# A four-layer graph network: the diagonal out of layer 1's gather lists, and layer 2 written between layer 1's blocks

## The chip, the cores and the metric

The kernel runs on one core of a Trainium2 chip. Times are device microseconds of one execution. Beside the timed runs there is one execution that the hardware profiler took; all durations of single instructions come from it.

## What is computed

Four residual layers over a graph of 2708 nodes with 128 features each, every one closed by a layer norm. `adj` is a 2708 x 2708 matrix of which some 0.6% of the entries are non-zero (16 per row on average); its diagonal is always filled.

```python
# layer 0: neighbours' mean, weighted
x = ln(x + (adj.T @ x) / adj.sum(axis=0)[:, None])
# layer 1: one message per pair (i, j), weighted by adj, then an update
s, d = x @ msg_w[:, :D].T, x @ msg_w[:, D:].T
agg = einsum('ijd,ij->id', gelu(s[:, None] + d[None] + msg_b), adj)
h = gelu(concat([x, agg], -1) @ upd_w.T + upd_b) + x
x = ln(x + ln(h))
# layer 2: a product with adj, batch statistics over the nodes, leaky relu
h = adj @ (x @ W) + b
x = ln(x + leaky(gamma * (h - h.mean(0)) * rsqrt(h.var(0) + eps) + beta))
# layer 3: four attention heads, scores masked and weighted by adj, row sums to one
x = ln(x + concat(heads(x, adj)) @ w)
```

The messages of layer 1 and the scores of layer 3 are needed only where `adj` is not zero.

## The kernel before

The nodes stand in 22 blocks of rows: 21 of 128 and one of 20.

**Layer 0 and the search.** `load` brings a block's rows (128 x 2708 numbers, 1.39 MB) through SP's queue into a ring of nine slots. `count_and_sum` counts the non-zeros of each row on ScalarE (two passes with an accumulated sum: signs, L401, and negatives, L404) and multiplies the block with x on TensorE (L411), summing over all blocks in six PSUM banks. `extract` finds the non-zero entries of the rows on VectorE: the eight largest of each of 16 segments (L435) with their places (L430), and from these 128 candidates the 32 largest, eight at a time. The first 13 blocks (`SPLIT`) are searched during layer 0, the other nine, the second group, during layer 1. The order of VectorE's instructions is written by hand up to the end of layer 0, and that of TensorE, VectorE and ScalarE in layer 3. In between, a planner of the language orders each engine's instructions: by their place in the text, and by when it expects their inputs to be ready.

**Lists.** `lists` turns the found keys into values and column numbers, `ranking` orders the nodes of a group by their number of neighbours, and `place` scatters the list of each node to its rank in an HBM table (`lists_dram`; GpSimd). `sorted_lists` reads them back, so that block b of layer 1 holds nodes of similar degree, and `CAPS[b]` bounds the length of the longest list in it. A wrong bound or an overfull list is counted in `wrong`, which chooses a dense path at the very end.

**Layer 1.** Layer 0 leaves x in `x1_dram` and d (with its bias) in `d_dram`. For each of the 22 sorted blocks `own_row` gathers the nodes' own x; `messages` gathers, for each place k of the lists, the row of d that place k names for each of the 128 nodes (one GpSimd instruction for each k, L237, into one of five buffers for up to eight of them), adds s, applies gelu and sums, weighted, on VectorE (L813, L816, L824); `update` does the rest, scatters the result to `x2_dram` and leaves x W of the block in SBUF (`xw`).

**Transposition.** Layer 2 sums over the columns of `adj`, in layer 1's order. So `transposed` turns each block of rows on TensorE (L877), evicts four 128 x 128 pieces at a time on ScalarE (L882, three buffers) and writes them to `at_dram` through SP's queue (L884): 154 writes. The second group's rows are still in the ring; the first group's are loaded again. In the text the second group is transposed after its search, one block after each block of layer 1 from block 0 on; the first group after blocks 9 to 12.

**Layer 2** stands after the loop. For each sorted block it gathers 128 rows of `at_dram` (GpSimd, into the ring) and multiplies them with `xw` on TensorE (L929), in six banks. Batch statistics, layer norm and the tables of layer 3 follow, then layer 3 over 24 blocks and 100 quads of gathers.

Of the kernel before, what the change touches and what calls it, by code (L numbers as in the profile page):

```python
# [9 lines left out]
FP = mybir.dt.float32  # L10
# [5 lines left out]
P = 128  # L16
# [18 lines left out]

SLOTS = 32
# [6 lines left out]
CAPS = [32, 24, 21, 20, 19, 18, 17, 16, 16, 15, 14, 13, 12, 31, 22, 20, 18, 17, 16, 14, 13, 10]  # L43
# [36 lines left out]
def gnn_resnorm_kernel(  # L80
# [123 lines left out]
    x1_dram = tables.tile([NBLK * P, D], FP, name="x1_dram")  # L204
    d_dram = tables.tile([NBLK * P, D], FP, name="d_dram")
# [10 lines left out]
    wrong = keep.tile([P, NBLK, 4], FP, name="wrong")  # L216
# [19 lines left out]
    def gather(dst, table, index):  # L236
        nc.gpsimd.indirect_dma_start(  # L237
            out=dst,
            out_offset=None,
            in_=table[0:N, :],  # L240
            in_offset=bass.IndirectOffsetOnAxis(ap=index, axis=0),
        )
# [85 lines left out]
    with ExitStack() as layer:  # L328
# [9 lines left out]
        nc.gpsimd.memset(cnt, 0.0)  # L338
        k1 = work.tile([P, NBLK, SLOTS], FP, name="k1")
# [58 lines left out]
        def count_and_sum(b, rows):  # L398
            r0, n = BLOCKS[b]
            junk = work.tile([P, N], I8, name="junk")  # L400
            nc.scalar.activation(  # L401
                junk[0:n, :], rows[0:n, :], AF.Sign, accum_out=cnt[0:n, b : b + 1]
            )
            nc.scalar.activation(  # L404
                junk[0:n, :], rows[0:n, :], AF.Relu, scale=-1.0,
                accum_out=wrong[0:n, b, 0:1],
            )
            for jb in ORDER:
                j0, m = BLOCKS[jb]
                for k, c0, f0, f1 in acc_parts(jb):  # L410
# [7 lines left out]
                    started.add(k)  # L418

# [94 lines left out]
        def lists(b0, b1):  # L514

            nb = b1 - b0
            shape = [P, nb, SLOTS]
# [4 lines left out]
            v1 = k1[:, b0:b1, :]  # L522
            nc.vector.tensor_copy(rows[:, :, 2 * SLOTS], cnt[:, b0:b1])
            nc.vector.tensor_copy(rows[:, :, 2 * SLOTS + 1], node[:, b0:b1])
            nc.vector.tensor_copy(code, k2[:, b0:b1, :])
# [5 lines left out]
            cols = rows[:, :, SLOTS : 2 * SLOTS]  # L531
# [7 lines left out]
            nc.vector.tensor_tensor(rows[:, :, 0:SLOTS], v1, seg.bitcast(FP), ALU.mult)  # L539
# [16 lines left out]
        def sorted_lists(g):  # L556
# [3 lines left out]
            for c0, c1, n in parts:  # L560
# [6 lines left out]
                nc.vector.tensor_copy(idx[0:n, c0:c1, :], ls[0:n, c0:c1, SLOTS : 2 * SLOTS])  # L567
# [25 lines left out]
        def spread(b, po, c0):  # L593
# [23 lines left out]
            nc.vector.tensor_scalar(bad[0:n], node3[0:n, b, 0:1], float(c), None, ALU.is_gt)  # L617
# [44 lines left out]
        for b in range(RING):  # L662
            take(b)
        for b in range(SPLIT):
# [39 lines left out]
        def layer0(b0, count, n):  # L704
# [32 lines left out]
            for j in range(count):  # L737
# [6 lines left out]
                x1_dram[b0 * P : b0 * P + w, :].rearrange("(b p) w -> p b w", p=n),  # L744
# [10 lines left out]
            for j in range(count):  # L755
# [10 lines left out]
                d_dram[b0 * P : b0 * P + w, :].rearrange("(b p) w -> p b w", p=n),  # L766
# [24 lines left out]
        def own_row(b):  # L791
            n = BLOCKS[b][1]
            x_s = mine.tile([P, D], FP, name="x_s", bufs=3)
# [1168 lines left out]
```

## Times and profile before

| | us |
|---|---|
| median of 3 runs (lowest to highest) | 1979.47 (1973.92 to 1994.36) |
| the profiled execution | 1674.75 |
| its span, first to last instruction | 1673.0 |
| layer 0: from the start to its last matmul | 190.5 |
| end of layer 0, tables of x and d | 190.5 to 224 |
| layer 1 with the transpositions and the first part of layer 2 | 224 to 831 |
| rest of layer 2's product | 831 to 882 |
| layer 2's statistics, tables of layer 3 | 882 to 951 |
| layer 3 | 951 to 1673 |

The stages overlap at their edges; the bounds are the last layer-0 matmul, the first gather of layer 1, the last gather before GpSimd falls idle, the last layer-2 matmul and the last scatter of layer 2's result. In the profile a gather or scatter is one GpSimd instruction named DMA_INDIRECT: its time is the time to issue, and the data land later. A matmul in float32 appears as two records. The granted clock is TensorE's, as a share of full speed.

### The profile page before, as it was taken

How to read it: one execution, taken by the hardware profiler on the slowest of the kernel's cores; microseconds unless marked ns; L12 is line 12 of the kernel's file. 1: busy time of each engine (PE TensorE's matmuls, PEld its weight loads, DVE VectorE, ACT ScalarE, POOL GpSimd, SP SyncE). 2: the span in 40 equal slices, each digit the busy share in tenths (PEclk: the TensorE clock that was granted, in tenths of full speed). 3: DMA queues.
4: the chain of work that ended last, by engine and by line, in shares of the span. 5: the costliest groups of instructions: out<-in, count | busy, mean ns of one | idle time of the engine just before them, and what ended most of it. 6: DMA issues, size and time to landing. Idle time of an engine off the chain costs nothing. (4 is left out here: it accounts for less than half of the span.)

```text
span 1673.0 us, 24020 instructions
## 1 busy us (share of the span) xinstructions
PE 1197.2 (72%) x5876; PEld 850.9 (51%) x5876; DVE 1215.7 (73%) x5697; ACT 695.7 (42%) x2635; POOL 916.7 (55%) x1007
## 2 busy tenths in 40 slices
PE   5996654455626544463795769988989988998994
PEld 5996543334414533463684325554555555555553
DVE  9999966777747571455444479788889888898883
ACT  4959543433314120111111534454545545554552
POOL 0000247777775677777610578665656666666530
PEclk9997555555555666686796856776677777767675
DMA  9433277798937524342531687976666766867630
GB/s 352 179 128 123 50 213 170 206 230 239 258 90 181 168 60 117 119 148 84 190 138 45 201 273 206 233 215 190 192 191 203 214 190 166 231 190 221 190 92 8
DMA packets 162245, 288.49 MB, mean 172 GB/s; under 512 B 44342, under 2 KB 115890, under 8 KB 155015
## 3 DMA queue, kind: packets, MB, share of 16 engines
q0 software_dynamic: 61120, 191.23, 40.8%
q1 hardware_dynamic: 95893, 90.69, 17.5%
q10 hardware_dynamic: 5082, 4.94, 1.0%
q8 instruction: 49, 0.80, 0.2%
q14 instruction: 101, 0.83, 0.2%
HBM read 242.74 MB, written 43.97 MB: 171 GB/s over the span
## 5 line engine op out<-in xcount | busy, mean ns | idle before, releaser
L237 POOL DMA_INDIRECT g<-t_dram,idx x400 | 402.3, 1006 | 195.1 <-issue 133.4
L237 POOL DMA_INDIRECT msg<-d_dram,idx x398 | 376.9, 947 | 124.6 <-issue 103.6
L1254 ACT ACTIVATE sum_junk<-g 126x128 bf16<-126x128 f32 (+3 forms) x800 | 235.3, 296 | 117.0 <-DVE g L1246 66.1
L929 PE MATMUL acc<-x_nat,at_rows 128*128 128x128 f32 (+2 forms) x968 | 155.5, 318 | 119.9 <-DMA at_rows<-at_dram,perm 119.9
L1223 PE MATMUL z<-x,copies 32*126 32x512 f32 (+3 forms) x800 | 212.3, 887 | 30.4 <-DVE g L1423 29.7
L877 PE MATMUL pt_a<-ident,rows 128*128 128x128 f32 (+1 forms) x484 | 115.6, 393 | 145.8 <-ACT at_sb L882 145.6
L929 PEld LDWEIGHTS acc<-x_nat,at_rows 128*128 128x128 f32 (+2 forms) x968 | 140.0, 225 | 130.7 <-DMA at_rows<-at_dram,perm 110.8
L1423 DVE TENSOR_TENSOR g<-g,z 126x1536 f32<-126x1536 f32 (+3 forms) x100 | 174.9, 1749 | 11.5 <-PE z L1223 11.3
L877 PEld LDWEIGHTS pt_a<-ident,rows 128*128 128x128 f32 (+1 forms) x484 | 82.3, 202 | 173.1 <-ACT at_sb L882 172.0
L411 PE MATMUL acc<-x_nat,rows 128*128 128x129 f32 (+5 forms) x1188 | 155.1, 290 | 18.5 <-DMA rows<-in_adj_dram 18.5
L1228 PE MATMUL z<-g,ident 126*126 126x512 f32 (+3 forms) x200 | 166.2, 926 | 0.0
L411 PEld LDWEIGHTS acc<-x_nat,rows 128*128 128x128 f32 (+2 forms) x1188 | 148.8, 207 | 24.5 <-DMA rows<-in_adj_dram 19.3
L1254 ACT ACTIVATION_READ_ACCUMULATOR sum_junk<-g 126x1 f32 (+3 forms) x800 | 149.6, 187 | 0.0
L1300 PEld LDWEIGHTS po_s<-wm,g 126*128 126x128 f32 (+3 forms) x800 | 119.4, 233 | 43.3 <-DVE wm L1287 32.1
L1300 PE MATMUL po_s<-wm,g 126*128 126x24 f32 (+6 forms) x800 | 121.3, 306 | 25.2 <-DVE wm L1287 23.4
L824 DVE SCALAR_TENSOR_TENSOR own<-msg,ls,own 128x128 f32<-128x128 f32 (+1 forms) x310 | 108.1, 349 | 37.9 <-ACT msg L816 36.5
L813 DVE TENSOR_TENSOR msg<-msg,own 128x1024 f32<-128x1024 f32 (+4 forms) x58 | 61.8, 1065 | 95.3 <-PE own L804 63.6
L245 POOL DMA_INDIRECT lists_dram<-lists,rank x22 | 21.5, 978 | 183.0 <-DVE cv L435 162.5
L1246 DVE SCALAR_TENSOR_TENSOR g<-g,a_ps 126x1024 f32<-126x1024 f32 (+3 forms) x100 | 121.2, 1212 | 0.2 <-issue 0.2
L882 ACT COPY at_sb<-pt_a 128x512 f32<-128x512 f32 (+3 forms) x154 | 69.5, 479 | 116.4 <-DMA at_dram<-at_sb 112.3
L430 DVE FIND_INDEX8 ci<-cv,rows 128x8 uint32<-128x170 f32 (+1 forms) x352 | 114.7, 326 | 0.0
L435 DVE MAX8 cv<-rows 128x8 f32<-128x170 f32 (+1 forms) x352 | 110.8, 318 | 0.0
(283 smaller groups left out, 2135.6 us busy)
## 6 DMA issues: line engine op xcount, KB each, us to landing
rows<-in_adj_dram SPq DMA_DIRECT2D x34, 1354.0 KB
at_dram<-at_sb SPq DMA_DIRECT2D x105, 256.0 KB
g<-t_dram,idx POOLq DMA_INDIRECT x400, 4.6
msg<-d_dram,idx POOLq DMA_INDIRECT x398, 3.0
t_dram<-t_row SPq DMA_DIRECT2D x21, 256.0 KB
at_dram<-at_sb SPq DMA_DIRECT2D x21, 64.0 KB
x_dram<-x_nat SPq DMA_DIRECT2D x5, 256.0 KB
d_dram<-d_sb SPq DMA_DIRECT2D x5, 256.0 KB
```

The source lines that it names most:

```text
L237: nc.gpsimd.indirect_dma_start(out=dst, out_offset=None, in_=table[0:N, :], in_offset=bass.IndirectOffsetOnAxis(ap=index, axis=0),)
L411: nc.tensor.matmul(accs0[k][0:m, c0 : c0 + f1 - f0], lhsT=rows[0:n, j0 : j0 + m], rhs=x_nat[0:n, b, f0:f1], start=k not in started, stop=( ...
L430: nc.vector.max_index(out=ci[0:n, at], in_max=cv[0:n, at], in_values=rows[0:n, c0 : c0 + cw])
L435: nc.vector.max(out=cv[0:n, 8 * s : 8 * s + 8], in_=rows[0:n, c0 : c0 + cw])
L877: nc.tensor.transpose(pt[0:m, j, 0:n], rows[0:n, c0 : c0 + m], ident[0:n, 0:n])
L929: nc.tensor.matmul(accs2[ib // 4][0:m, (ib % 4) * D : (ib % 4 + 1) * D], lhsT=at[0:n, i0 : i0 + m], rhs=xw[0:n, b, :], start=(b == 0 and i ...
L1223: nc.tensor.matmul(z3[0:e, r, :] if r < 3 else z1[0:e], lhsT=copies[g][rows, j, :], rhs=own[b][1][rows, :], start=True, stop=r < 3, skip_g ...
L1228: nc.tensor.matmul(z1[0:e], lhsT=ident[0:e, 0:e], rhs=g4[0:e, 3, 0:HD], start=False, stop=True, skip_group_check=True,)
L1246: nc.vector.scalar_tensor_tensor(z, z, 0.0, a_ps[0:e].unsqueeze(1).to_broadcast((e, 2, HD)), ALU.max, ALU.mult)
L1254: nc.scalar.activation(junk[0:e], g4[0:e, r, hd * D : (hd + 1) * D], AF.Identity, accum_out=sc[0:e, r, hd : hd + 1],)
L1300: nc.tensor.matmul(po[:, p0 * HEADS : (p0 + g) * HEADS], lhsT=g4s[i][0:e, r, HD : HD + D], rhs=wm[0:e, 4 * i + r, :, :], start=True, stop= ...
L1423: nc.vector.tensor_tensor(z, z, z3[0:e], ALU.add)
```

## The change

It has three parts.

1. The diagonal leaves the lists. `count_and_sum` first multiplies the diagonal block of the rows, then sets its diagonal to zero on GpSimd (`affine_select`) and only then counts; `extract` finds one entry less per row. The diagonal's values are read from HBM by a DMA of single elements on ScalarE's queue (`diag`), and `lists` puts them into place 0, with the node itself as the column. In layer 1 the message of place 0 needs no gather: x and d of a node now stand side by side in one table, `dx_dram`, so the gather of the own row brings d along; the other gathers read the same table as rows of half the length, with doubled numbers. `CAPS` now bounds the lists without the diagonal.
2. `transposed` comes before `extract` for the second group and puts the diagonal back: for the diagonal block two accumulated matmuls, the cleared block and a diagonal matrix made on ScalarE. The first group's blocks are reloaded and transposed one after each layer-1 block from the second on, two after blocks 9 to 11.
3. Layer 2's product moves into layer 1's loop: from block 11 on, up to two of its blocks after each `update`; only the last stands behind the loop.

Besides there is a check that no diagonal entry is negative.

```diff
-CAPS = [32, 24, 21, 20, 19, 18, 17, 16, 16, 15, 14, 13, 12, 31, 22, 20, 18, 17, 16, 14, 13, 10]
+CAPS = [30, 22, 20, 19, 18, 17, 16, 15, 15, 14, 13, 12, 10, 29, 20, 18, 17, 16, 14, 13, 12, 8]
...
-            for jb in ORDER:
+            for jb in [b, *(jb for jb in ORDER if jb != b)]:
...
+                if jb == b:
+                    nc.gpsimd.affine_select(
+                        out=rows[0:n, j0 : j0 + m], in_=rows[0:n, j0 : j0 + m],
+                        compare_op=ALU.not_equal, fill=0.0, base=0,
+                        pattern=[[-1, m]], channel_multiplier=1,
+                    )
+            junk = work.tile([P, N], I8, name="junk")
+            nc.scalar.activation(
+                junk[0:n, :], rows[0:n, :], AF.Sign, accum_out=cnt[0:n, b : b + 1]
+            )
...
             take(b)
+            if b == 3:
+                line = adj[0:1, 0:1]
+                for b0, count, n in ((0, NFULL, P), (NFULL, 1, NREM)):
+                    nc.scalar.dma_start(
+                        diag[0:n, b0 : b0 + count],
+                        bass.AP(
+                            tensor=line.tensor, offset=line.offset + b0 * P * (N + 1),
+                            ap=[[N + 1, n], [P * (N + 1), count], [1, 1]],
+                        ),
+                    )
...
-            x_s = mine.tile([P, D], FP, name="x_s", bufs=3)
-            gather(x_s[0:n, :], x1_dram, perm[0:n, b : b + 1])
+            x_s = mine.tile([P, 2, D], FP, name="x_s", bufs=3)
+            gather(
+                x_s[0:n].rearrange("p t d -> p (t d)"), dx_dram, perm[0:n, b : b + 1]
+            )
...
+            mk = x_s[0:n, 0, :]
+            nc.vector.tensor_tensor(mk, mk, s_ps[0:n], ALU.add)
+            nc.scalar.activation(mk, mk, AF.Gelu)
+            weigh(0, mk)
+            for c0, c1 in chunks_of(kk):
...
                 for k in range(kc):
-                    gather(msg[0:n, k, :], d_dram, idx[0:n, b, c0 + k : c0 + k + 1])
+                    gather(
+                        msg[0:n, k, :], dx_dram.rearrange("n (t d) -> (n t) d", t=2),
+                        idx[0:n, b, c0 + k + 1 : c0 + k + 2], rows=2 * N,
+                    )
...
+            if cleared:
+                back = small.tile([P, P], FP, name="back")
+                nc.scalar.activation(back, ident, AF.Copy, scale=diag[:, b : b + 1])
...
+                    if cleared and j0 + j == b:
+                        for i, part in enumerate((rows[0:n, c0 : c0 + m], back[0:n, 0:m])):
+                            nc.tensor.matmul(
+                                pt[0:m, j, 0:n], lhsT=part, rhs=ident[0:n, 0:n],
+                                start=(i == 0), stop=(i == 1),
+                            )
...
+        def layer2(b):
+
+            n = BLOCKS[b][1]
+            at = ring.tile([P, N], FP, name="at_rows", tag="rows")
+            gather(at[0:n, :], at_dram, perm[0:n, b : b + 1])
+            for ib in range(NBLK) if b == 0 else ORDER:
+                i0, m = BLOCKS[ib]
+                nc.tensor.matmul(
+                    accs2[ib // 4][0:m, (ib % 4) * D : (ib % 4 + 1) * D],
+                    lhsT=at[0:n, i0 : i0 + m],
+                    rhs=xw[0:n, b, :],
+                    start=(b == 0 and ib % 4 == 0),
+                    stop=(b == NBLK - 1 and ib in (3, 7, 11, 15, 19, 20)),
+                )
...
                     e = left.pop(0)
+                    transposed(e, rows_of[e], True)
                     run(extract(e, rows_of[e]))
-                    transposed(e, rows_of[e])
...
             update(b, x_s, x_st, agg)
-            if not left and b >= 9:
-                for e in range(4 * (b - 9), min(SPLIT, 4 * (b - 8))):
+
+            for _ in range(2 if b in (9, 10, 11) else 1):
+                if b and again:
+                    e = again.pop(0)
                     transposed(e, load(e))
-
-
-        accs2 = banks("acc2_")
-        for b in range(NBLK):
...
+            if b == 11:
+                accs2.extend(banks("acc2_"))
+            if b >= 11:
+                for e in range(2 * (b - 11), min(b, 2 * (b - 10))):
+                    layer2(e)
+        layer2(NBLK - 1)
```

## The prediction

> **What bounds the kernel now.** I read the windows first, by stage, then GpSimd's timeline in the stage that the change is about, then TensorE's and VectorE's at that stage's two ends. The chain of waits is of no use: it holds only the last scatter. A line of the windows gives the stretch, its length, busy time and count of TensorE, its weight loads, VectorE, ScalarE and GpSimd, then granted clock, DMA share and GB/s.
>
> ```profile
> 0.00:190.50 190.50, 155.24 (x1192) 148.85 (x1193) 185.11 (x1075) 137.63 (x121) 15.34 (x71) 0.91 0.47 175
> ...
> 224.00:515.00 291.00, 142.46 (x611) 109.78 (x610) 195.78 (x1030) 108.29 (x248) 217.85 (x229) 0.56 0.78 204
> 515.00:831.00 316.00, 164.24 (x912) 144.89 (x911) 162.17 (x745) 62.35 (x157) 224.79 (x238) 0.67 0.44 126
> 831.00:882.00 51.00, 50.65 (x378) 44.85 (x377) 23.00 (x109) 8.28 (x27) 7.31 (x11) 0.94 0.40 159
> ```
>
> Layer 0 (to 190 us) is VectorE's: 185 of 190. Layer 1 (224 to 831) seems only 71 to 75% GpSimd's, but its timeline leaves no room between gathers:
>
> ```profile
> 641.46 0.95 POOL L237 DMA_INDIRECT msg<-d_dram,idx  x1 [0.30 <-issue]
> 642.71 0.94 POOL L237 DMA_INDIRECT msg<-d_dram,idx  x1 [0.30 <-issue]
> 643.96 0.94 POOL L237 DMA_INDIRECT msg<-d_dram,idx  x1 [0.30 <-issue]
> ```
>
> Start to start is 1.25 us: 0.94 of work and 0.30 of issue. So layer 1 is counted in slots. From 224 to 831 GpSimd runs 398 message gathers, 22 own rows, 19 scatters of results, 9 of lists and 18 gathers of A^T rows: 466 slots x 1.25 = 582 us of 607. The other 25 us are stalls, of which some 12 stand in one place, where the second group's lists come late:
>
> ```profile
> 514.17 0.94 POOL L237 DMA_INDIRECT msg<-d_dram,idx  x1 [0.31 <-issue]
> 520.73 0.94 POOL L237 DMA_INDIRECT x_s<-x_dram,perm  x1 [5.62 <-DMA at_dram<-at_sb]
> 524.49 1.00 POOL L245 DMA_INDIRECT lists_dram<-lists,rank  x1 [2.82 <-DVE rs_y L277]
> 528.30 0.90 POOL L245 DMA_INDIRECT lists_dram<-lists,rank  x1 [2.82 <-DMA lists_dram<-lists,rank]
> ```
>
> After the last message gather at 825.90 seven of layer 2's 22 row gathers are still to come. From 831 to 882 TensorE is full (50.65 of 51 us): it works off layer 2, whose last stretch is this one; layer 2's statistics start behind it.
>
> ```profile
> 867.75 13.70 PE L929 MATMUL acc<-x_nat,at_rows 128*128 128x128 f32 x94
> ```
>
> Layer 2 needs 155 us of TensorE altogether; 92 of them run from 548 to 800 and 63 after that. Layer 3 (951 to 1673, TensorE busy for 622 of 722) is not touched: its lists keep 32 places, the diagonal now in the first, and each degree falls by one, so the order of the nodes stays.
>
> **The Trainium skill.** "Perfetto Trace Analysis", Identifying the Most-Contended Engine, calls occupancy a fair measure for GpSimd. Here it is not: 72% busy and yet full, by the 0.30 us of issue in each slot. "DMA: Bandwidth & Descriptors", SWDGE vs HWDGE vs iDMA, says that GpSimd computes the descriptors of its DMAs in software. The trace agrees: the cost follows the instruction, not the bytes (947 ns for 128 message rows of 512 B, 948 for 128 rows of A^T of 10.8 KB). "TensorE: Matmul & The Clock Gate", What's actually happening, says that TensorE's clock is halved by default and released by activity; the windows agree (0.56 in layer 1's first half, 0.94 where TensorE is full).
>
> **The change part by part**, in us of the profiled execution (1674.75, span 1673.0).
>
> *Layer 0: diagonal cleared on GpSimd.* VectorE's first search starts at 9.77, as soon as its small tables are done; TensorE's first adjacency matmul starts only at 15.67. Now the search of block 0 must wait for the two matmuls that read the diagonal block (0.23 each) and for the select. The trace has such a select once, on the identity: 0.28. So VectorE starts at 15.67 + 0.46 + 0.28 + about 0.4 of hand-over = 16.8, **7 us later**. VectorE has no gap after that until the end of layer 0, so the 7 us go through. For later blocks TensorE is far ahead (8 blocks in the 50 us from 50 to 100, against VectorE's 13 us per block), so the other 21 selects are off the path; all sit in a GpSimd queue that is empty before 166.
>
> *Diagonal read from HBM, on ScalarE's queue.* 2708 pieces of 4 bytes. The nearest row is the load of x: 2560 rows hold that queue for 9.78 us. Behind it stand ScalarE's counts, whose nearest reader is the ranking; it ends at 154.84 and is read at 162.45. That slack of 7.6, plus VectorE's own shift of 7, covers 10. I take 0, with 10 as the upper end; no gain is possible.
>
> *Layer 1: message gathers 398 to 368* (sum of the caps: 237 to 221 in the first group, 161 to 147 in the second). 30 slots x 1.25 = **-37.5**. Own-row gathers carry 1 KB instead of 512 B and stay one slot each. VectorE gains 30 x (0.35 + 0.13) = 14 and pays 22 x (0.28 add + 0.35 weigh) = 14: even. ScalarE pays 22 x 0.28. The nine extra scalings (0.27) and second matmuls of the transpositions are under 6 us, beside gathers. The lists get two copies of 0.16 per call: 1 us, taken as nothing.
>
> *Transpositions.* The same 154 evictions and 154 writes, and 13 reloads on SP's queue. They run at 2.0 us per write (224 to 535), DMA-paced: ScalarE waits 112 us for the writes in all. In the new text the last one stands at block 11, in the old one at block 12; the planner already had them done by 542. I expect 535 to 550: no gain.
>
> *Layer 2 behind the blocks.* From block 11 on two row gathers follow each block, so that at the last message gather only blocks 20 and 21 are left. Five or six slots move ahead of that gather: **+7**. What then follows is the last update and little layer 2. Before, it took from 825.9 to 881.4, or 55.5. I build the new one from the trace: 3 to land, 8 for the two last chunks on VectorE (843.04 to 850.6), about 12 for an update that finds TensorE free (830.15 to 841.7 for the part on VectorE alone), 2 for the transposed product, and 44 matmuls of 0.146 = 6.4, with as much again for a neighbour that is still running: some 36. **-20**; between -30 (only block 21 is left) and 0 (the planner places them as before).
>
> The sum is 7 - 37.5 + 7 - 20 = **-43.5**: 1631 us for a profiled execution. The median of the three timed runs lies 305 us above the profiled one, and nothing on the page says where. I carry this distance over as it is: 1979.5 - 43.5 = **1936**.
>
> **Rivals.**
> *Half clock.* If the distance of 305 us is TensorE at half clock throughout, layer 2's pile at the end was dearer in the timed runs: a block takes 9.8 us at 0.5 (22 matmuls in 4.88 from 540 to 560) against 5.7 at 0.93 (148 in 19.28). Ten blocks' worth of matmuls ran after 800: 10 x 4 = 40 us more to hide, and layer 0 would be TensorE's, so that the 7 us are hidden too. That gives -43.5 - 40 + 7 = -77: 1903. For it: layer 3 runs at 0.70, so half clock there could give most of the 305. Against it: no run shows it.
> *The lists are the next bound.* The first group saves 16 gathers, 20 us; if the second group's searches end no earlier (514 before, 521 now), the stall at 514 grows by those 20 us and by the 7. What is left is -43.5 + 20 + 7 = -16.5: 1963. For it: VectorE stood still for 21 us from 481 to 502 behind a ScalarE that waited for A^T writes. Against it: the searches have no input that the gathers delay, and VectorE is busy for only 196 of 291 us.
> *Slower: GpSimd stands before layer 2's first gather.* That gather reads what all 154 writes leave; GpSimd works its queue in order, so every message behind it waits too. GpSimd gets there after 231 + (211 + 12 + 11 + 9) x 1.25 = 535. If the writes end at 542 as before, it costs 7; it eats the whole gain when they end after 579, that is at 2.3 us per write instead of 2.0. With reloads competing from block 1 on and DMA engines 78% busy that is possible; ending at 600 gives +22: 2001.
> *The change doesn't do what it says:* the planner places layer 2's gathers as before. Then -37.5 + 7 = -30: 1949, inside the main range.
>
> **How the numbers follow.** Main case, with the placing as before in it: 0.52 (1912 to 1957). Half clock 0.2, lists 0.15, GpSimd standing 0.13. The range runs from 1893 (half clock with a shorter tail) to 1978 (lists with the diagonal's 10 us and a little noise), which leaves out the slower case and the lowest part of half clock. One per cent, 20 us, is what a measurement of this kernel can tell (its three runs spread over 20). Faster by over 1% (below 1959.7): 0.52 + 0.2 + a third of the lists' case, less a little for noise: 0.75. Within: 0.13. Slower: 0.12.
>
> **What would show it.** Right: 368 message gathers, still 1.25 us apart; VectorE's first search near 17; the stretch from the last message gather to the last layer-2 matmul near 36 us; layer 3 as long as now. Wrong: a GpSimd gap before the first gather of A^T rows (the slower case), a stall over 25 us at the second group's lists, or layer-2 gathers still bunched behind the last message.

## The result, and the profile after

The changed kernel takes 1992.6 us in the median beside 1987.3 for the kernel before: **1.0037 of it, 95% interval 1.0018 to 1.0057**. The forecast was 1936. The same instructions take about 2000 us in some comparisons (1983 to 2020 for the kernel before) and about 1670 in others (1669 to 1674), on one chip even both (2019.9 and later 1669.5), so times are compared within a comparison only and the two are called the 2000 level and the 1670 level below. The profile that the forecast was read from was taken at the 1670 level, the three runs beside it at the 2000 level; the profile of the changed kernel (span 1988.3) is again one of the 2000 level. In the profiles, idle time of an engine just before an instruction is called a stand below.

The windows of the changed kernel, cut at the second group's last list scatter, the last message gather and the last layer-2 matmul (length; busy time and count of TensorE, weight loads, VectorE, ScalarE, GpSimd; clock, DMA share, GB/s):

```profile
0.00:203.80 203.80, 160.07 (x1192) 153.16 (x1193) 185.53 (x1079) 138.10 (x123) 21.61 (x94) 0.89 0.45 163
239.00:622.00 383.00, 150.10 (x638) 115.50 (x637) 207.76 (x1103) 115.75 (x276) 205.89 (x217) 0.56 0.58 161
622.00:1003.00 381.00, 191.35 (x1005) 167.44 (x1005) 151.40 (x658) 54.40 (x142) 207.27 (x220) 0.64 0.35 112
1003.00:1070.00 67.00, 49.95 (x245) 41.20 (x245) 24.48 (x118) 10.13 (x33) 5.82 (x10) 0.68 0.08 27
```

Layer 0 ends 13 us later (203.8 against 190.5) with the same 185 us of VectorE work. GpSimd is busy for 206 of 383 and 207 of 381 us, 54% where it was 71 to 75%. The end, 51 us of full TensorE before, is 67 us with TensorE busy for 50. GpSimd's timeline in layer 1's second half shows that the slot is as it was and what stands beside it:

```profile
907.09 0.94 POOL L238 DMA_INDIRECT x_s<-dx_dram,perm  x1 [14.70 <-PE acc L944]
908.34 0.94 POOL L238 DMA_INDIRECT msg<-dx_dram,idx  x1 [0.30 <-issue]
909.59 0.94 POOL L238 DMA_INDIRECT msg<-dx_dram,idx  x1 [0.30 <-issue]
```

Messages are 1.25 us apart, but the own-row gather waited 14.7 us. The view names layer 2's matmuls (`PE acc`) as what ended that wait. They are not what took the time: TensorE itself had stood for 14.9 us shortly before, behind a copy on ScalarE.

```profile
896.49 0.80 PE L898 MATMUL tail<-w_l,x_nt 128*128 128x128 f32 x2 [14.88 <-ACT x_nt L896]
896.17 0.27 ACT L896 COPY x_nt<-tail 128x128 f32<-128x128 f32 x1 [22.38 <-remote]
ACT x_nt L896 <- remote: 103.2, 7, 22.4
```

What the copy reads was written by 881.6 (TensorE's transposition at 881.23 takes 0.37), yet ScalarE started it at 896.17. The matmuls of the update that frees the gather's buffer stand behind it in TensorE's queue (at 903.48 to 905.71). `remote` is the view's word for a wait that ends with a semaphore event for which it finds no recorded instruction. The last line sums such stands before this copy from 234 to 1070 us: 103.2 us in 7 places. The profile of the same kernel at the 1670 level has none on ScalarE in layers 1 and 2.

TensorE's timeline at the end, which answers to the full TensorE of before:

```profile
1044.74 3.91 PE L944 MATMUL acc<-x_nat,at_rows 128*128 128x128 f32 x22 [0.35 <-ACT x_nat L899]
...
1057.83 0.26 PE L894 MATMUL tail<-ident,x_n 20*128 20x20 f32 x1 [4.51 <-DVE x_n L312]
...
1059.32 10.16 PE L944 MATMUL acc<-x_nat,at_rows 20*128 20x128 f32 x44 [0.35 <-ACT x_nat L899]
```

Layer 2's pile is gone; what remains waits for the updates of the last blocks, one after the other.

### The profile page after: what moved, and what is told of

It is laid out like the page before. It is cut to its first block, busy times and chain, and to the rows that moved or that the text cites. A ratio compares the mean times of both kernels' runs of the same rounds, so it can differ in the third digit from the quotient of the medians.

```text
span 1988.3 us, 24119 instructions
## 1 busy us (share of the span) xinstructions
PE 1276.3 (64%) x5903; PEld 901.4 (45%) x5903; DVE 1224.3 (62%) x5717; ACT 701.8 (35%) x2663; POOL 894.5 (45%) x1000
## 2 busy tenths in 40 slices
DMA packets 164355, 288.03 MB, mean 145 GB/s; under 512 B 46584, under 2 KB 118102, under 8 KB 157125
## 5 line engine op out<-in xcount | busy, mean ns | idle before, releaser
L238 POOL DMA_INDIRECT msg<-dx_dram,idx x368 | 347.8, 945 | 179.8 <-issue 145.4
L944 PE MATMUL acc<-x_nat,at_rows 128*128 128x128 f32 (+2 forms) x968 | 178.5, 340 | 89.5 <-issue 61.3
L944 PEld LDWEIGHTS acc<-x_nat,at_rows 128*128 128x128 f32 (+2 forms) x968 | 157.7, 244 | 105.9 <-issue 77.6
L921 PE MATMUL pt_a<-ident,rows 128*128 128x128 f32 (+2 forms) x475 | 108.1, 379 | 138.7 <-ACT at_sb L926 61.4
L406 PE MATMUL acc<-x_nat,rows 128*128 128x129 f32 (+4 forms) x1188 | 159.6, 295 | 23.0 <-DMA rows<-in_adj_dram 23.0
L1354 PE MATMUL po_s<-wm,g 126*128 126x24 f32 (+6 forms) x800 | 133.6, 324 | 48.6 <-DVE wm L1341 44.9
L921 PEld LDWEIGHTS pt_a<-ident,rows 128*128 128x128 f32 (+2 forms) x475 | 78.7, 195 | 160.8 <-ACT at_sb L926 74.2
L1277 PEld LDWEIGHTS z<-x,copies 32*126 32x126 f32 (+3 forms) x800 | 65.5, 250 | 113.7 <-issue 67.8
L1292 DVE SCALAR_TENSOR_TENSOR g<-z,a 126x128 f32<-126x128 f32 (+3 forms) x400 | 91.9, 286 | 31.9 <-remote 15.3
L238 POOL DMA_INDIRECT x_s<-dx_dram,perm x22 | 21.0, 956 | 176.7 <-PE acc L944 53.5
```

The costliest lines, as they stand in the source:

```text
L238: nc.gpsimd.indirect_dma_start(out=dst, out_offset=None, in_=table[0:rows, :], in_offset=bass.IndirectOffsetOnAxis(ap=index, axis=0),)
L406: nc.tensor.matmul(accs0[k][0:m, c0 : c0 + f1 - f0], lhsT=rows[0:n, j0 : j0 + m], rhs=x_nat[0:n, b, f0:f1], start=k not in started, stop=( ...
L921: nc.tensor.transpose(pt[0:m, j, 0:n], rows[0:n, c0 : c0 + m], ident[0:n, 0:n])
L944: nc.tensor.matmul(accs2[ib // 4][0:m, (ib % 4) * D : (ib % 4 + 1) * D], lhsT=at[0:n, i0 : i0 + m], rhs=xw[0:n, b, :], start=(b == 0 and i ...
L1277: nc.tensor.matmul(z3[0:e, r, :] if r < 3 else z1[0:e], lhsT=copies[g][rows, j, :], rhs=own[b][1][rows, :], start=True, stop=r < 3, skip_g ...
L1354: nc.tensor.matmul(po[:, p0 * HEADS : (p0 + g) * HEADS], lhsT=g4s[i][0:e, r, HD : HD + D], rhs=wm[0:e, 4 * i + r, :, :], start=True, stop= ...
```

## The experiments

Two theories came first. A: the shorter lists bring what was forecast, and layer 2's new place gives it back on TensorE. B: outside the profile that the forecast used, GpSimd is not the bound, and fewer gathers are worth nothing.

### The parts, beside a kernel before of 2019.9 us

**The kernel before again**, unchanged.

> The kernel before, once more with a profile. If the profile of before that the prediction was made from was an execution out of the ordinary, this one has a span near 1985 us, layer 3 takes some 830 us (as in the profile after) instead of 711, and layer 2's last matmul ends near 1065 instead of 881. If the profile after is the odd one, this one is near 1675 again.

Measured: 2019.95, span 2018.2, granted clock 0.669 (0.700 in the profile of before). Layer 0 takes what it took: its last matmul starts at 190.6 (190.5 in the profile of before), the first message gather at 227.9 (227.7). Behind it the last message gather comes at 1012.3 instead of 825.9, and from layer 3's first gather to the end it takes 844 us instead of 711. Between first and last message GpSimd issues the same 459 instructions, but stands still for 209 us beyond its 0.30 per instruction, 22 in the profile of before. So the distance between the two levels (345 us between these two profiles) lies in layers 1 to 3 alone, and for GpSimd it is stands. ScalarE shows them as well: its waits between first and last message that end in `remote` add up to 260 us here and to none in the profile of before.

**Part 1 alone**: the lists without the diagonal; transpositions and layer 2 in their old places.

```diff
+                    run(extract(e, rows_of[e]))
                     transposed(e, rows_of[e], True)
-                    run(extract(e, rows_of[e]))
...
-            for _ in range(2 if b in (9, 10, 11) else 1):
-                if b and again:
-                    e = again.pop(0)
+            if not left and b >= 9:
+                for e in range(4 * (b - 9), min(SPLIT, 4 * (b - 8))):
                     transposed(e, load(e))
-            if b == 11:
-                accs2.extend(banks("acc2_"))
-            if b >= 11:
-                for e in range(2 * (b - 11), min(b, 2 * (b - 10))):
-                    layer2(e)
-        layer2(NBLK - 1)
+        accs2.extend(banks("acc2_"))
+        for b in range(NBLK):
+            layer2(b)
```

> Part 1 alone: the diagonal out of the lists, with the old text order of transposition and of layer 2. Theory A (the 30 gathers saved are worth their 37 us, and the new place of layer 2 on TensorE gives them back): near 1950. Theory B (in ordinary executions GpSimd is not the bound of layer 1, so that fewer gathers are worth nothing): 1985 to 1995.

Measured: 1989.7, 0.986 (0.9789 to 0.9931). From the first to the last message 740.5 us instead of 784.5.

**Parts 2 and 3 alone**: the kernel before with the new order of transpositions and layer 2 between the blocks, lists as they were.

> Parts 2 and 3 alone: lists as before, transposition ahead of the search and spread, layer 2 between layer 1's blocks. Theory A: 2020 to 2030, what part 1 gains on top. Theory B: 1985 to 1995.

Measured: 2017.0, 0.9972 (0.9946 to 0.9998). The messages take 18 us longer (802.5), the end from the last message gather to the last layer-2 matmul 26 us less (42.7 against 68.3). That is just under what A expects (2020 to 2030): by itself the new order costs nothing here. If it takes back what the lists bring, it does so only together with them.

**Parts 1 and 2**: the changed kernel with layer 2 behind the loop.

> The changed kernel with layer 2's product written behind the loop again. Theory A: near 1955, as with the lists alone. Theory B: about 1990, no change.

Measured: 1994.5, 0.987 (0.9808 to 0.9933). B falls: fewer gathers pay at the 2000 level too, though GpSimd stands there for a quarter of the time. The stands come on top of the slots and do not hide them: with 30 gathers fewer (37.5 us of slots) the lists alone send their messages in 44 us less, with 202 us of stands instead of 209. Part 2 is worth nothing that can be seen (0.987 with, 0.986 without).

### Own-row buffers, beside a kernel before of 1987.1 us

The gather of block b+1's own rows writes the buffer that `update` of block b-2 reads. Are the three buffers what GpSimd stands at?

> The changed kernel itself, beside the kernel before on one chip. Theory A (layer 2's place between layer 1's blocks gives back what the shorter lists bring: its two products per block stand in TensorE's queue ahead of the block's own small matmuls): 1.000 to 1.008 of the kernel before, that is some 20 to 30 us above the lists alone (0.986) and above the change with layer 2 behind the loop (0.987). Theory B (the parts' results and the whole's only differ because they were measured beside different executions of the kernel before): 0.985 to 0.99, no more than 5 us from the change with layer 2 behind the loop.

The changed kernel: 1999.6, 1.0042 (1.0004 to 1.008), the first result once more. As a share of its kernel before it lies above the same change with layer 2 behind the loop (0.987; intervals apart). But the two stood in two comparisons, whose kernels before differ by 33 us, and their own times are only 5 us apart (1999.6 and 1994.5). With three buffers the two never stood in one comparison at the 2000 level, so this alone does not show what layer 2's place costs there.

The other three have one edit each, in the lists alone, the changed kernel and the kernel before:

```diff
-            x_s = mine.tile([P, 2, D], FP, name="x_s", bufs=3)
+            x_s = mine.tile([P, 2, D], FP, name="x_s", bufs=6)
```

> The diagonal out of the lists alone (0.986 of before) with six buffers in place of three for a block's own rows of x and d. In the ordinary executions GpSimd stands for 8 to 15 us in front of the own-row gather of most blocks, where the profile forecast from showed nothing; the gather for block b+1 writes the buffer that the update of block b-2 reads last. Theory A (the three buffers hold GpSimd up): these stands go, some 100 us of them, and 30 to 90 us of time: 0.94 to 0.97 of before. Theory B (a chain over TensorE, ScalarE and VectorE sets the period of a block, and GpSimd only waits at whichever buffer is the first to be full): the stands move to the message gathers, and the time stays within 8 us of the lists alone: 0.982 to 0.99.

> The changed kernel with six own-row buffers. Theory A (buffers): GpSimd no longer waits for layer 2's matmuls at the own-row gathers of blocks 16 to 20 (12 to 15 us each), and the kernel gains 40 to 100 us on its three-buffer twin: 0.95 to 0.98 of before. Theory B (chain): TensorE still has both products of layer 2 ahead of a block's small matmuls, so the period of 33 us per block from block 15 on stays, and the time stays within 8 us of its twin.

> The kernel before with six own-row buffers. Theory A (buffers): 40 to 100 us faster, 0.95 to 0.98. Theory B (chain): 0.995 to 1.003. If the gain here is as large as in the lists alone with six buffers, GpSimd's 30 slots are worth their 37 us whatever else happens; if this kernel gains more than that one, the shorter lists had only relieved the same wait.

Measured: lists alone 1958.9, 0.9861 (0.983 to 0.9892); changed kernel 1970.1, 0.9882 (0.9856 to 0.9909); before 1980.4, 0.9954 (0.9932 to 0.9976). For the lists alone B holds, as far as two comparisons can tell (0.986 with three buffers, beside 2019.9). GpSimd's timeline of the lists alone with six buffers shows why:

```profile
776.27 0.94 POOL L238 DMA_INDIRECT msg<-dx_dram,idx  x1 [13.30 <-issue]
...
785.12 0.95 POOL L238 DMA_INDIRECT x_s<-dx_dram,perm  x1 [0.30 <-issue]
```

The own row no longer waits here, a message does. Summed between first and last message, own rows stand for 37 us instead of 120 with three buffers, messages for 108 instead of 67, scatters of results for 28 instead of 5, those of lists for 22 instead of 10; the total is 195 instead of 202. The changed kernel gains 1.6% all the same, within this one comparison. Its profiled execution took 1990.1 us, 20 more than the median and among the two longest of its twenty, so it does not show where the gain lies; that stays open.

### Layer 2's products and layer 0, beside a kernel before of 1673.7 us

> The kernel before, profiled beside these three, to have an ordinary execution of it on the same chip. As in the last profile of it: span near the timed median, last message gather near 1000, last layer-2 matmul near 1070, layer 3 some 830 us. A span near 1673 again would mean that the short executions come back and belong to the kernel, not to one moment.

Measured: 1676.1, span 1674.3. All runs of this comparison were at the 1670 level, and the window of layer 2's end shows the full TensorE of the profile of before:

```profile
831.00:882.00 51.00, 50.68 (x381) 45.20 (x379) 23.46 (x112) 9.05 (x29) 7.30 (x11) 0.94 0.41 162
```

So the short execution belonged neither to the kernel nor to the profiler.

Half of layer 2's matmuls left out, in the changed kernel and, as control, in the one with layer 2 behind the loop:

```diff
-            for ib in range(NBLK) if b == 0 else ORDER:
+            for ib in range(NBLK) if b == 0 else ORDER if b == NBLK - 1 else ORDER[::2]:
```

> The changed kernel with every second matmul of layer 2's product left out for the 20 blocks between the first and the last (about 80 us of TensorE); the gathers stay. Theory A (layer 2's products in TensorE's queue ahead of a block's small matmuls make GpSimd stand before the own-row gathers of blocks 16 to 20): the stands of 12 to 15 us there fall to under 8, the period of 33 us falls to 28 or less, and the kernel gains 25 to 50 us on itself: 0.978 to 0.992 of before. Theory B (the order of GpSimd's own queue costs the time, with layer 2's gathers ahead of messages): stands and period as in the full kernel, a gain of 5 to 12 us from a shorter end alone: 0.997 to 1.001.

> The same matmuls left out of the change with layer 2 behind the loop (0.987 in full): the control. Theory A: its products stand in nobody's way, so it gains only what the end of layer 2 shrinks by, 5 to 15 us: 0.980 to 0.985, less than half of what the changed kernel gains. Theory B: the same gain in both.

Measured: 1648.0, 0.9846 (0.9803 to 0.989), and 1665.6, 0.9944 (0.9924 to 0.9965). With all matmuls the two kernels stand at 0.9939 and 0.9931 (below). Leaving half of them out is worth 0.9% between the blocks and nothing behind the loop, though in two comparisons at the same level. A holds, with less than it forecast: between the blocks TensorE pays for them. In the profiles, own-row gathers whose wait ends with a layer-2 matmul stand for 13.8 us in the changed kernel (1670 level), for 5.5 with half of the matmuls and for 3.2 in the kernel before. Behind the loop the end does not get shorter: the last layer-2 matmul ends 60.9 us after the last message gather with half of the matmuls and 57.9 with all. The updates of the last blocks come one after another at the same times (scatters of results at 837.5, 852.2 and 864.6; with all matmuls at 837.8, 852.8 and 864.2), and so they, and not the number of matmuls, set this end.

In the lists alone with six own-row buffers, block 0's diagonal segment searched next to last:

```diff
-            for s, (c0, cw) in enumerate(SEGS):
+            turn = [*range(1, NSEG - 1), 0, NSEG - 1] if b == 0 else list(range(NSEG))
+            for i, s in enumerate(turn):
+                c0, cw = SEGS[s]
...
```

> The diagonal out of the lists alone, six own-row buffers, and for block 0 the segment that holds the diagonal block searched next to last, so that VectorE's first search needs no cleared diagonal. If the late first search goes through to the end as forecast, VectorE begins near 10 us instead of 16.8, the first message gather comes 6 to 8 us earlier than with the same kernel's usual order (240), and the time falls by as much: 0.981 to 0.984 of before. If the later blocks or the tables take it back: first gather still near 238 and 0.985 to 0.988.

Measured: 1664.6, 0.9944 (0.9917 to 0.9971), and the first message gather at 240.5, no earlier than without. The search began at 9.90, but VectorE then stood for 4.5 us at block 1's diagonal and for 7.8 at the load of the diagonal, until 44.4. The changed kernel's VectorE timeline shows the second wait there too:

```profile
16.78 0.58 DVE L444 MAX8 cv<-rows 128x8 f32<-128x170 f32 x2 [6.79 <-POOL rows L415]
...
44.74 0.19 DVE L997 TENSOR_SCALAR wrong<-diag 128x22 f32<-128x22 f32 x1 [5.86 <-DMA diag<-in_adj_dram]
```

The check for a negative diagonal, last in the text, was planned straight behind the load that it reads. The load of single elements is issued at 28.8 and lands by 44.7; what comes off the first wait is added to the second.

### The whole change at the 1670 level, beside a kernel before of 1669.5 us

> The changed kernel on one more chip. The kernel before takes 1674 us on one chip so far and 1987 to 2020 on the others, with the same instructions. Theory A (on the chips that take 2000 us engines stand still at places where on the other they do not, so that layer 2's products in TensorE's queue only cost there): 1.003 to 1.006 if the kernel before takes some 2000 here, 0.985 to 0.995 if it takes some 1674. Theory B (the change is worth nothing on either kind): 0.999 to 1.006 on both.

Measured: 1658.7, **0.9939 (0.9917 to 0.9961)**.

> The change with layer 2 behind the loop, beside the changed kernel on one chip. On a chip of 2000 us: Theory A 0.984 to 0.992, that is 20 to 35 us under the changed kernel; Theory B the same as the changed kernel within 6 us. On a chip of 1674 us: Theory A 0.992 to 1.000, some 5 to 15 us over the changed kernel, since the products then fill TensorE's free time and shorten the end.

Measured for the change with layer 2 behind the loop: 1658.0, 0.9931 (0.9898 to 0.9964), the same. The profiled executions are not equally typical: the changed kernel's (1652.5) was its quickest of twelve, that with layer 2 behind the loop (1665.1) its second longest of eight. The next table sums GpSimd's timelines: instructions and stands (idle time beyond 0.30 each) from the first message gather to the second group's last list scatter, from there to the last message gather, and the end up to the last layer-2 matmul.

| | first gather at | first part: us, instructions, stands | second part: us, instructions, stands | end |
|---|---|---|---|---|
| before, 1670 | 227.8 | 302.1, 228, 15.8 | 296.3, 231, 7.1 | 56.2 |
| changed, 1670 | 236.6 | 292.1, 216, 20.1 | 296.7, 219, 22.1 | 43.4 |
| layer 2 behind, 1670 | 240.4 | 293.4, 216, 21.6 | 281.1, 214, 12.8 | 57.5 |
| before, 2000 | 227.9 | 405.0, 228, 118.9 | 379.4, 231, 90.2 | 68.3 |
| changed, 2000 | 239.2 | 382.4, 216, 111.2 | 380.9, 219, 107.0 | 66.6 |
| layer 2 behind, 2000 | 240.0 | 388.8, 216, 117.8 | 363.4, 214, 95.4 | 65.4 |

Of the rows of the 2000 level, the first and the last belong to the comparison with 2019.9, the middle one to that with 1987.3, for which no profile of the kernel before was taken.

Layer 2's place costs the second part 16 us at the 1670 level (five instructions more and 9 us of stands) and gives 14 back at the end. At the 2000 level, across the two comparisons, it costs 18 and gives nothing back. The lines for it: GpSimd's own rows of blocks 19 to 21 in the changed kernel at the 1670 level, then the same blocks with layer 2 behind the loop.

```profile
747.18 0.94 POOL L238 DMA_INDIRECT x_s<-dx_dram,perm  x1 [5.47 <-PE acc L944]
...
775.27 0.94 POOL L238 DMA_INDIRECT x_s<-dx_dram,perm  x1 [8.36 <-PE acc L944]
...
796.71 0.92 POOL L238 DMA_INDIRECT x_s<-dx_dram,perm  x1 [0.30 <-issue]
```

```profile
758.66 0.94 POOL L238 DMA_INDIRECT x_s<-dx_dram,perm  x1 [0.30 <-issue]
...
781.27 0.94 POOL L238 DMA_INDIRECT x_s<-dx_dram,perm  x1 [2.85 <-PE own L829]
...
805.19 0.92 POOL L238 DMA_INDIRECT x_s<-dx_dram,perm  x1 [5.42 <-PE own L829]
```

And TensorE before such a gather, changed kernel, 1670 level and then 2000 level:

```profile
742.26 0.80 PE L944 MATMUL acc<-x_nat,at_rows 128*128 128x128 f32 x2 [11.01 <-DMA at_rows<-at_dram,perm]
...
747.08 10.58 PE L944 MATMUL acc<-x_nat,at_rows 128*128 128x128 f32 x82
757.49 0.27 PE L894 MATMUL tail<-ident,x_n 128*128 128x128 f32 x1
```

```profile
906.99 9.06 PE L944 MATMUL acc<-x_nat,at_rows 128*128 128x128 f32 x61
916.29 0.27 PE L944 MATMUL acc<-x_nat,at_rows 128*128 128x128 f32 x1 [0.24 <-issue]
917.02 0.36 PE L944 MATMUL acc<-x_nat,at_rows 128*128 128x128 f32 x1 [0.46 <-issue]
919.13 0.38 PE L944 MATMUL acc<-x_nat,at_rows 128*128 128x128 f32 x2 [1.75 <-issue]
...
932.38 0.42 PE L894 MATMUL tail<-ident,x_n 128*128 128x128 f32 x1
```

At 742 TensorE has stood for 11 us in front of a product whose rows had not landed, and the small matmuls of the block (at 743.57 to 746.65) queue behind it. At the 2000 level two products take 25.4 us (906.99 to 932.38) where 10.4 do at 1670, since TensorE stops between single matmuls for no reason that the profile shows (here TensorE stands, in the result's lines ScalarE did); the transposition of x_n, and with it the update, comes that much later.

Two measures against layer 0's waits, the early search above and this one, which checks the diagonal where `lists` has it anyway:

```diff
             nc.vector.tensor_copy(rows[:, :, SLOTS], node[:, b0:b1])
+            nc.vector.tensor_scalar(wrong[:, b0:b1, 4], rows[:, :, 0], 0.0, None, ALU.is_lt)
...
-        nc.vector.tensor_scalar(wrong[:, :, 4], diag, 0.0, None, ALU.is_lt)
```

> The changed kernel with one part undone: the check for a negative diagonal no longer reads the diagonal straight after its load, at 44 us in VectorE's queue, but from the lists, where it lies anyway. Theory A (this check makes VectorE, and so the whole of layer 0, wait 6 us for the load of single elements, a second wait after that of the first search): the first message gather comes 5 to 6 us earlier than the changed kernel's 239 to 240, and the time falls by 4 to 8 us, 0.2 to 0.4%. Theory B (layer 0's delay is all from the first search): first gather unchanged within 1 us, time the same.

Measured in the changed kernel: 1660.7, 0.9954 (0.9937 to 0.9971), first message gather at 236.3 against 236.6. The wait at 44 is gone, and layer 0's last matmul starts at 199.1 instead of 203.0, yet the first gather comes no earlier. The granted clock takes the 4 us in between. From 215 to 236 us, where TensorE computes d, it was 0.81 in the changed kernel's profile and 0.56 in this one (length, TensorE, weight loads, VectorE, ScalarE, GpSimd, clock, DMA share, GB/s):

```profile
215.00:236.00 21.00, 16.51 (x102) 13.66 (x103) 20.52 (x110) 10.84 (x38) 1.69 (x2) 0.81 0.62 172
215.00:236.00 21.00, 17.90 (x85) 15.25 (x86) 17.24 (x91) 8.22 (x28) 1.94 (x2) 0.56 0.54 150
```

The matmuls for d took 275 ns in the median in the first and 421 in the second, and VectorE waited for them for 0.5 us and for 3.8. Three other profiles of the 1670 level with both waits in layer 0 had 0.50 there and their first gather at 240.3 to 240.8; beside those, moving the check brings 4 us. The time shows no gain (1660.7 beside 1658.7).

> The diagonal out of the lists alone, six own-row buffers, block 0's diagonal segment searched next to last (alone worth nothing: VectorE then stood longer at the check of the diagonal) and the check in the lists. Theory A (both waits in layer 0 must go before either counts): first message gather near 230, 10 us earlier than with the first of the two measures alone, and 5 to 10 us less time: 0.978 to 0.984 of before on a chip of 2000 us, 0.986 to 0.991 on one of 1674. Theory B (layer 0 is late for another reason, more work on VectorE): first gather at 238 or later, 0.986 and 0.994.

Measured, with both measures in the lists alone with six own-row buffers: 1650.3, **0.989 (0.9858 to 0.9921)**, the first gather at 233.3 against 240.5 with the early search alone, own rows without any stand. It is under both kernels, though the intervals touch.

### Both mends on the whole change, beside a kernel before of 1982.8 us

> The whole change with the three mends: six own-row buffers, block 0's diagonal segment searched next to last, the check of the diagonal in the lists. On a chip at 1670 us the changed kernel's messages lost 14 us to GpSimd standing before the own-row gathers of blocks 18 to 20 behind layer 2's matmuls, and its end was 13 us shorter than before; with layer 2 behind the loop it was the other way round, at the same time. Theory A (the stands come from the three buffers, the shorter end from layer 2's place: with six both gains stand together): end from the last message gather to the last layer-2 matmul under 46, stands at own rows under 5, and 5 to 15 us under the lists alone with the same mends: 0.978 to 0.986 of before. Theory B (layer 2's matmuls cost the same time wherever they stand, TensorE being the one who pays): within 4 us of the lists alone with the mends, 0.987 to 0.992. At 2000 us: A 0.97 to 0.98, B 0.984 to 0.99.

> The diagonal out of the lists alone with the same three mends, beside the one above on one chip: as measured, 0.989 of before at 1670 us (0.986 to 0.992); at 2000 us 0.978 to 0.986, the shorter lists bringing more there.

Measured, each with six own-row buffers, the early search and the check in the lists: 1968.8, 0.9896 (0.986 to 0.9931), in the whole change, and 1948.6, **0.9835 (0.9776 to 0.9893)**, in the lists alone, with layer 2 behind the loop and the old order of transpositions. The end is 58.9 against 65.9 us, the messages take 754.7 against 731.0. Neither theory holds: the whole change is neither under the lists alone (A) nor within 4 us of them (B), but 20 us above. Within one comparison layer 2's place thus costs some 20 us at this level with six buffers, though the two intervals overlap by 0.3%; with three buffers only the two comparisons say so.

## Why the prediction was wrong, by its steps

Two steps failed; the larger one lies in the sum.

**"30 slots x 1.25 = -37.5", with GpSimd's stands left as they were.** At the 1670 level, where the sum was made, the whole change is worth -10.8 us in the median (1658.7 beside 1669.5), against -43.5: 33 of the forecast us do not exist even there. The slots came off as forecast, 30.0 us of them up to the last message. But 19.4 us of new stands took two thirds of that back, and nothing had been set down for stands.

**"I carry this distance over as it is."** At the 2000 level the change is worth +5, another 16 us off. The distance is no constant that lies beside the kernel: it consists of stands in the engines' own queues in layers 1 to 3. That layer 2's place costs more there than at the 1670 level is seen with six buffers (20 us in one comparison; at the 1670 level only the kernels with three buffers were compared, and they take the same). For the kernel of the result itself it is inferred from two comparisons. Against it stands that the new order alone cost nothing beside 2019.9 (0.9972). What makes up the +5 us stays open, since the kernel before has no profile beside 1987.3, and the chip may have its part in it.

**The terms**, at the 1670 level, from the profiles of before (span 1674.3) and of the changed kernel (1650.7, its quickest run):

| step | forecast | measured |
|---|---|---|
| layer 0, start of the messages | +7 | +8.8 here, +12.5 to +13.0 in three other profiles of this level |
| slots up to the last message | -37.5 + 7 = -30.5 | 459 to 435: -30.0 |
| stands of GpSimd up to there | as before | 22.8 to 42.2: +19.4 |
| end of layer 2 | -20 | 56.2 to 43.4: -12.8; about 0 at 2000 |
| layer 3 | as long as now | -8.3 here; -1.2 in the kernel with layer 2 behind |

Two entries owe something to the granted clock. Layer 3 ran at 0.72 in this profile of the changed kernel and at 0.70 in that of before, with TensorE busy for 608 and 617 us, and the matmuls for d took 275 ns in the median here and 421 in that of before, which is worth 4 us at the first gather (above). An estimate without the two, -23.6 + 8.3 + 4, is -11, the -10.8 of the medians.

*Layer 0* ends 12.5 us later (its last matmul starts at 203.0 instead of 190.5). The wait for the select was right (forecast 16.8, measured 16.78). The term that failed is the load of the diagonal, "I take 0, with 10 as the upper end": its readers were sought on ScalarE, and the one that waits is the check on VectorE. The description of the change names this check; the prediction gave it no line.

*Slots.* 368 gathers, 1.25 us apart, 30 slots less and five gathers of A^T rows moved ahead of the last message (15 before, 20 after): as forecast.

*Stands.* In the first part the twelve instructions fewer are 15 us; the late start takes 8.8 of them and the longer stands 4.3, so that the second group's last lists go out at 528.7 instead of 529.9. The rival "the lists are the next bound" forecast a stand longer by 27 us there, and 4.3 are seen; where the messages start at 240.3 to 240.8, the lists go out at 533.8 to 534.6, so they follow the start. In the second part twelve fewer are again 15 us, and 15.0 more of stands take them all, 10 of these at own rows, behind layer 2's matmuls.

*The end.* The pieces that the forecast lists add up to 37.8, not 36. More weighs that it has one update behind the last message, where two whole ones follow at the 1670 level (scatters at 842.3 and 857.7, after one at 827.8 that was almost done) and three at 2000 (1028.7, 1043.0 and 1058.0). The kernel before had three as well, beside a TensorE that was full:

```profile
842.29 1.01 POOL L245 DMA_INDIRECT x_dram<-x_n,perm  x1 [11.63 <-DVE x_n L311]
...
855.41 1.00 POOL L245 DMA_INDIRECT x_dram<-x_n,perm  x1 [8.37 <-DVE x_n L311]
...
866.80 0.93 POOL L245 DMA_INDIRECT x_dram<-x_n,perm  x1 [9.18 <-DVE x_n L311]
```

So taking layer 2's pile away could not shorten the end to one update. Besides, the last block's 44 matmul records take 10.2 us instead of 6.4.

*Transpositions*: the last write is issued at 533.7 instead of 535.8, and the first gather of A^T rows did not wait: the slower rival falls. *Half clock* falls too: 0.67 against 0.70, and a layer-2 matmul of 340 ns against 318. *The planner places as before* was half true: with layer 2 behind the loop GpSimd's order is that of the changed kernel up to block 14, and 16 of 22 row gathers stand ahead of the last message.

## What to carry to other kernels

Before a sum from one execution is laid on a time from another, ask whether both ran alike: here the profile's own time was 15% under the timed one, and the difference was standing time in the very queues that the change touches. A slot that is saved pays only up to the next wait, so recount the stands in each half of a stage, not the busy time alone. A profile names what ended a wait, not what made it long: follow the named engine one step further back. Moving work into a queue's free time pays only if its data have landed when its turn comes; whatever is queued behind it waits as well, and a check that reads a slow load can hold a whole engine although nobody needs its answer.

## What the runs showed of the hardware

The same program, with the same 24119 instructions, 164355 DMA packets and 288.03 MB, took 1650.7 and 1988.3 us. These are the page's lines for all engines (busy time, share of the span, count), for layer 3's gathers and for layer 2's matmuls (busy time, mean ns, then idle time before them and what ended most of it), of the changed kernel at the 1670 level and at the 2000 level:

```profile
PE 1187.0 (72%) x5903; PEld 846.2 (51%) x5903; DVE 1216.3 (74%) x5717; ACT 701.5 (42%) x2663; POOL 896.9 (54%) x1000
...
L238 POOL DMA_INDIRECT g<-t_dram,idx x400 | 403.4, 1009 | 186.1 <-issue 135.6
...
L944 PE MATMUL acc<-x_nat,at_rows 128*128 128x128 f32 (+2 forms) x968 | 159.9, 328 | 99.4 <-DMA at_rows<-at_dram,perm 98.4
```

```profile
PE 1276.3 (64%) x5903; PEld 901.4 (45%) x5903; DVE 1224.3 (62%) x5717; ACT 701.8 (35%) x2663; POOL 894.5 (45%) x1000
...
L238 POOL DMA_INDIRECT g<-t_dram,idx x400 | 402.7, 1007 | 306.1 <-issue 220.3
...
L944 PE MATMUL acc<-x_nat,at_rows 128*128 128x128 f32 (+2 forms) x968 | 178.5, 340 | 89.5 <-issue 61.3
```

VectorE, ScalarE and GpSimd work for the same time within 1%. TensorE is busy for 7.5% longer, at a granted clock of 0.672 instead of 0.719. The rest is stands, among them many for which the views name neither an instruction nor a transfer (`issue`, `remote`): between first and last message ScalarE stands for 218 us before `remote` at the 2000 level and not at all at the 1670 level. Layer 0 is free of them (190.5 and 190.6 us to its last matmul in the kernel before). The stands keep to places of the program: in layer 3 the step from the ninth quad of gathers to the tenth takes 6.6 us in all nine profiles of the 1670 level and 25 to 32 in all eleven of the 2000 level, while 42 to 46 of the 99 steps stay under 5.3 us there (48 to 56 at the 1670 level). One chip showed both levels at different times. What sets the level, and what holds the engines at these places, stays open; no run varied either.
